# A two-layer vision tower: late rankings, layer 1's attention with its second pair beside the first, and another order of the feed-forward's pieces and end

## The chip, the cores and the metric

The kernel runs on one core of one Trainium2 chip. A core has a matrix engine (TensorE, PE in the profile, its weight loads are PEld), a vector engine (VectorE, DVE), a scalar engine (ScalarE, ACT), GpSimd (POOL) and SyncE (SP), which here only starts transfers. Each takes its instructions from a queue of its own and waits on semaphores for what others make. The metric is the device time of one execution in microseconds (us), as a median over runs.

## What is computed

A batch of 32 images of 3 x 256 x 256 goes through a tokenizer and two layers. All is float32; every image has N = 256 tokens of D = 256 features.

```python
h = L0_tok(x)                                  # 16 x 16 patches @ W.T + b
h = h + L0_attn(layernorm(h))                  # gated attention, relu(q k)^2
h = h + L0_ffn(layernorm(h))                   # the 127 best-ranked tokens of an image get a gelu MLP
h = h + L1_attn(layernorm(h))                  # phase memory
h = h + L1_ffn(layernorm(h))                   # experts' attention by head, two norms, two gates
```

Layer 0's feed-forward ranks each image's tokens by one weight, takes the best 127, and adds back `y * weight` at their places. Layer 1's attention makes phases for key and query, `tanh(gelu(x W1) W2) * freq * pi`, and reads a causal memory; for a fixed position it is a masked product:

```python
key_phasor = cos(key_phase) + 1j * sin(key_phase)
query_conj = cos(query_phase) - 1j * sin(query_phase)
memory     = cumsum(key_phasor[..., None] * V[:, :, None, :], axis=1)
retrieved  = real(sum(memory * query_conj[..., None], axis=2)) / sqrt(positions * K)
out        = x + layernorm(retrieved) @ Wo + bo
```

Layer 1's feed-forward works on 4 heads of 64 features with 4 experts each: causal softmax attention by head and expert, a gate over the experts, a residual, a norm, a two-layer MLP with a residual, a second norm, and a gate over the heads.

## The kernel before

The 32 images stay on the chip in `H[b]`, 128 partitions by 2 x 256. The stages follow one another: tokenizer (a), layer 0's attention (b, by pairs of images), layer 0's feed-forward (c, by quads), layer 1's attention (d, by pairs) and layer 1's feed-forward (e, by image). All matmuls go through `mm` (line 115) into one pool of eight PSUM banks, so TensorE's rows mostly carry L115; transposes have L188, L229, L482, L750 and L1254.

The order is written out by hand: `manual_schedule` makes every engine's queue follow the order of the Python calls. A stage is a loop over steps `t`, in which each piece of work of each unit is called at its own step; so work of several units is interleaved.

**Stage b's end and stage c.** `norms_c(b0)` normalizes a pair of images and makes the ranking weights `cw` (L378, VectorE). `turn_weights` (L482) turns `cw` on TensorE, and `ranks` (L389 to L400) counts ranks on VectorE and scatters the rows by GpSimd transfers. The rankings of the last two pairs fall into stage c's first two steps. Stage c takes four steps for a quad: `hidden_c` twice (16 matmuls each), `made` twice, `turn_c`, then `fetch` (GpSimd gathers result rows into `cx`, L816, two images each time) and `update` (VectorE adds them to `H`, L827, with the statistics that follow). `ORDER_C` sets the steps; `step_c(t)` calls what is due. The last quad's `fetch` and `update` fall behind stage c's loop (`END_C` = 32) and are called within stage d.

**Stage d**, a pair u in three steps: `norm_d` at 3u (VectorE, L774 to L777, tile `dx`, or `cx` for a pair that is normalized in stage c), `turn` at 3u+1 (8 transposes) and `residual_d` (GpSimd, four adds), `hidden` at 3u+2 (16 matmuls with gelu), `phases` at 3u+3 (16 small matmuls, two tanh, three VectorE steps L899 to L903 on `dz`, one sine), `match` at 3u+4 (16 small matmuls, then the causal mask on VectorE into `dat`, L919), `memory` at 3u+5, `output` at 3u+6 (16 matmuls, statistics L943, a power on GpSimd L149), `add_output` (L952) and `stats_e` at 3u+7. There are 16 pairs.

**Stage e**, an image b: six steps per image, at even steps `scores` (TensorE) with `weights` (VectorE adds the causal mask L1100, ScalarE the exponential L1102), at odd ones `values` (three calls, at 11, 13 and 15 of an image's own steps; copied out at L1118). All else of an image is cut into pieces `prep` and `post`, and the table `PIECES` gives each its step from the image's beginning; `EARLY` puts two ahead of the weights. The pieces of `post`: 0 to 2 the experts' gate (L1163 to L1177, then two multiplications on GpSimd, L1180), 3 the mixed sum (L1185 to L1188), 15 and 4 its squares and norm (ScalarE, L1193, GpSimd L1131 and L1132), 5 the scaling (L1198), 6 transposes (`fxT`), 16 a count of zeros, 7 the first MLP matmul, its relu `hx`, and four transfers that put `fxT` and `hx` into `both` (SyncE, L1215 and L1217), 8 the second matmul (`W`, L1226), 9 and 10 the second norm, 11 the scaling `enorm` and head gate (L1234 to L1241), 12 and 13 transposes there and back, 14 the output `fout` (L1259, L1263) with its transfer (L1264). Most of these tiles have one buffer. `LAST` sets how many steps the loop runs on after the last image has begun.

The loop before, in the few lines that set the order:

```python
for t in range(3 * (B // 2 - 1) + 8):          # stage d
    ...
    do(1, turn)
    do(7, add_output)
    ...
    if 3 <= t <= 5:
        step_c(END_C + t - 3)
...
for t in range(-1, 6 * (B - 1) + LAST):        # stage e
```

Of the kernel before, what the change touches and what calls it, by code (L numbers as in the profile page):

```python
# [33 lines left out]
F32 = mybir.dt.float32  # L34
# [6 lines left out]
P = 128  # L41
B, N, D = 32, 256, 256
NC = N // P
# [36 lines left out]
def vit_tower(tc, a, out):  # L80

    nc = tc.nc
# [62 lines left out]
    def pow_rstd(o, var):  # L145

        n = o.shape[1]
        nc.gpsimd.tensor_scalar(o, var, 1.0, 1e-5, ALU.mult, ALU.add)
        nc.gpsimd.tensor_tensor(o, o, minus_half[:, 0:n], ALU.pow)  # L149
# [254 lines left out]
    with (  # L404
# [71 lines left out]
        def turn_weights(b0):  # L476
            p = bank()
            for j in range(2):
                w = normed_c[b0][j][1]
                for c in range(NC):  # L480
                    o = j * N + c * P
                    nc.tensor.transpose(p[:, o : o + P], w[:, c : c + 1].to_broadcast([P, P]), ident)  # L482
            return p

        def ranks(b0, p):
            for j in range(2):
                rank_c(b0 + j, *normed_c[b0][j], p[:, j * N : (j + 1) * N])
# [301 lines left out]
    with region_c:  # L789
        st_d = new_stats("d")  # L790

        def hidden_c(b0, s, half):
            if half == 0:
                s.hT = p2.tile([P, 8, 4 * P], F32, name="hT")
            for m in range(4 * half, 4 * half + 4):
                p = bank()
                for k in range(2):
                    mm(p, w1[:, k, m * P : (m + 1) * P], s.xsel[:, k, :], k == 0, k == 1)
                nc.scalar.activation(s.hT[:, m, :], p, AF.Gelu_apprx_tanh, bias=col("b1", m))

        def made(b0, s, half):
            for j in range(2 * half, 2 * half + 2):
                p = bank()
                for m in range(8):
                    mm(p[:, 0:D], s.hT[:, m, j * P : (j + 1) * P], w2[:, m, :], m == 0, m == 7)
                y = p2.tile([P, D], F32, name="cy", bufs=4)
                nc.vector.tensor_tensor(y, p[:, 0:D], row_c("b2"), ALU.add)
                nc.sync.dma_start(results[b0 + j][:], y)

        def fetch(b0, s, half):  # L810
            s.y = s.y if half else []
            for b in range(b0 + 2 * half, b0 + 2 * half + 2):
                y = px.tile([P, NC, D], F32, name="cx", bufs=8)
                for c in range(NC):
                    k = b * NC + c
                    nc.gpsimd.indirect_dma_start(  # L816
                        y[:, c, :], None, results[b][:], bass.IndirectOffsetOnAxis(rank_of[:, k : k + 1], 0)
                    )
                s.y.append(y)

        def update(b0, s, half):
            for j in range(2 * half, 2 * half + 2):
                b = b0 + j
                st, rs, i = at(st_d, b)
                for c in range(NC):
                    k = b * NC + c
                    nc.vector.scalar_tensor_tensor(  # L827
                        H[b][:, c, :], s.y[j][:, c, :], w_kept[:, k : k + 1], H[b][:, c, :], ALU.mult, ALU.add
                    )
                    stats(st, i, c, H[b][:, c, :])  # L830
            pow_rstd_of(st_d, b0 + 2 * half, 2)

        ORDER_C = ((0, hidden_c, 0), (1, hidden_c, 1), (2, made, 0), (-1, turn_c, 0), (-8, first_ranks, 0),
                   (3, made, 1), (4, fetch, 0), (5, fetch, 1), (5, update, 0), (6, update, 1))

        def step_c(t):
            for at_step, do, j in ORDER_C:
                u, r = divmod(t - at_step, 4)  # L840
                if r == 0 and 0 <= u < B // 4 and (u > 1 or do is not first_ranks):
                    do(4 * u, quads[u], j)

        END_C = 4 * (B // 4 - 1) + 4
        pairs = [Pair() for _ in range(B // 2)]
        preparing = prepare()
        for t in range(END_C):
            if t < 2:
                ranks(B - 4 + 2 * t, turn_weights(B - 4 + 2 * t))
            if t == 0:  # L850
                norms_c(B - 2)
                residuals_c(B - 2)
            if t == END_C - 2:
                norm_d(0, pairs[0], px, "cx", 8)
            step_c(t)
            if t >= 8:
                next(preparing, None)
        passing.close()
# [5 lines left out]
    with (  # L864
# [4 lines left out]
            s.xT = p2.tile([P, 2, 2 * N], F32, name="dxT")  # L869
            transposed(s.xT, s.xs, copy_split)  # L870

        def hidden(b0, s, i):

            g = p2.tile([P, 2, 2 * N], F32, name=f"dg{i}")
            for m in range(2):
                p = bank()
                for k in range(2):
                    mm(p, (wk1, wq1)[i][:, k, m * P : (m + 1) * P], s.xT[:, k, :], k == 0, k == 1)
                nc.scalar.activation(g[:, m, :], p, AF.Gelu, bias=bias_d[:, 2 * i + m : 2 * i + m + 1])
            s.g = (s.g if i else []) + [g]  # L880

        def phases(b0, s):

# [48 lines left out]
                nc.scalar.copy(m.rearrange("p k n -> p (k n)"), p)  # L932
                s.m.append(m)

        def output(b0, s):
            st_m = spool.tile([P, 2 * NC, 2], F32, name="d_st")
            s.po = []
            for q in range(2 * NC):
                m, c, p = s.m[q // NC], q % NC, bank()
                for k in range(2):  # L940
                    mm(p, m[:, k, c * P : (c + 1) * P], wvo[:, k, :], k == 0, k == 1)
                six = spool.tile([P, 6], F32, name="six")
                nc.vector.bn_stats(six, p[:, 0:D])  # L943
                nc.vector.bn_aggr(st_m[:, q, :], six)
                s.po.append(p)
            s.rs = spool.tile([P, 2 * NC], F32, name="d_rs")
            pow_rstd(s.rs, st_m[:, :, 1])

        def add_output(b0, s):
            for q, p in enumerate(s.po):  # L950
# [8 lines left out]

        for t in range(3 * (B // 2 - 1) + 8):
            def do(step, which, *more):
                u, r = divmod(t - step, 3)
                if r == 0 and 0 <= u < B // 2:
                    which(2 * u, pairs[u], *more)

            do(1, turn)
            do(7, add_output)
            if t != 4:  # L970
                do(4, match)
            do(7, stats_e)
            do(1, residual_d)
            do(2, hidden, 0)
            if t == 5:
                match(0, pairs[0])
            do(2, hidden, 1)
            do(5, memory)
            do(3, phases)
            if t:  # L980
                do(0, norm_d, p8, "dx", 4)
            do(6, output)
            if 3 <= t <= 5:
                step_c(END_C + t - 3)
    right_d.close()
    passing_x.close()
    by_hand.close()
# [2 lines left out]
    with (  # L990
# [166 lines left out]
        def post(b, im, i):  # L1157
# [113 lines left out]


        images = [Image() for _ in range(B)]
        SCORES, VALUES, LAST = 6, 11, 46
        EARLY = ((32, post, 9), (22, post, 15))
        PIECES = (
            (0, prep, 0), (42, post, 12), (30, post, 16), (18, post, 1),
            (25, post, 5), (7, prep, 7), (31, post, 8), (19, post, 2),
            (26, post, 6), (44, post, 13), (2, prep, 2),
            (45, post, 14), (33, post, 10), (21, post, 3),  # L1280
            (28, post, 7), (40, post, 11),
            (23, post, 4), (17, post, 0), (-1, prep, -1),
        )

        def pieces(t, table):
# [6 lines left out]
        with order:  # L1292
            for t in range(-1, 6 * (B - 1) + LAST):
                active = [(images[b], t - 6 * b) for b in range(B)]
                if t % 2 == 0:
                    step = [(im, i - SCORES) for im, i in active if SCORES <= i < SCORES + 6]
                    made = [(im, i // 2 - 2) for im, i in active if i in (4, 6)]
                    for im, k in step:
                        scores(im, k)
                        scores(im, k + 1)  # L1300
                    for im, hp in made:
                        experts(im, hp)
                    for im, i in active:
                        if i == 6:
                            head_values(im)
                    pieces(t, EARLY)
                    for im, k in step:
                        weights(im, k)
                        weights(im, k + 1)
                    for im, hp in made:  # L1310
                        experts_out(im)
                pieces(t, PIECES)
                for im, i in active:
                    if i in (VALUES, VALUES + 2, VALUES + 4):
                        values(im, (i - VALUES) // 2)


        n_bad = p1.tile([P, 2], F32, name="n_bad")
# [390 lines left out]
```

## Time and profile before

The time is 2002.92 us (median of three runs, 2000.7 to 2003.91); the profiled execution has a span of 2000.3 us at a mean TensorE clock of 0.984.

| engine | busy us | share of the span |
|---|---|---|
| PE | 1942.6 | 97% |
| DVE | 1289.7 | 64% |
| ACT | 824.6 | 41% |
| POOL | 722.7 | 36% |

The stages on the trace's clock: a to about 196, b to about 692, c to about 934, d to about 1285, e to the end. In the loop of stage e an image takes about 20.5 us.

In a list of waits, the row names who waited, for whose work, then the time in all, how often, and the longest. In an answer in order of time, the columns are start, duration, engine, line, operation, output and inputs, shapes and count; a bracket at the end holds the idle time before it and what ended it. In a table by stretches, each engine has its busy time with the number of instructions, then come the mean granted TensorE clock, the share of the transfers' engines and the GB/s. "PEclk" on the page is that clock in tenths, in 40 equal slices.

### The profile page before, as it was taken

The page shows a single profiled execution, that of the slowest core. Times are in us where ns is not written, and L with a number is a line of the kernel's source. Part 1 is how long each engine was busy: PE and PEld are TensorE (multiplying, and loading weights), DVE is VectorE, ACT ScalarE, POOL GpSimd, SP SyncE. Part 2 cuts the span into 40 slices and gives each one's busy share as a digit, 9 for nine tenths or more (in the row PEclk, how much of TensorE's full clock was granted, in tenths as well). Part 3 has the DMA queues.
Part 4 walks back from the last instruction along what each step waited for, and adds up shares of the span by engine and source line. Part 5 has one row for each costly group of instructions (what it writes and reads, how often), then busy time and mean ns, then how long its engine had stood idle before and what let it go on. Part 6 is the DMA issues. An engine that isn't in the chain of part 4 may idle for free.

```text
span 2000.3 us, 37646 instructions
## 1 busy us (share of the span) xinstructions
PE 1942.6 (97%) x15108; PEld 1373.5 (69%) x15108; DVE 1289.7 (64%) x3605; ACT 824.6 (41%) x1549; POOL 722.7 (36%) x692
## 2 busy tenths in 40 slices
PE   9999999999999999998999999999999999999984
PEld 7886676666767666765555555577777777777762
DVE  2334566656565735334655646567889998989986
ACT  0002222222121111122344444377777777777761
POOL 1223234334342334234333342214443444444353
PEclk9999999999999999999999999999999999999995
DMA  8540000000000232121000000001222121212211
GB/s 297 158 142 1 0 19 29 24 14 22 11 21 11 85 98 80 52 68 50 11 1 1 0 1 1 6 18 44 49 53 57 44 65 44 60 49 58 52 50 54
DMA packets 69812, 95.08 MB, mean 48 GB/s; under 512 B 8576, under 2 KB 51200, under 8 KB 69248
## 3 DMA queue, kind: packets, MB, share of 16 engines
q1 hardware_dynamic: 62912, 75.04, 13.2%
q0 software_dynamic: 6144, 16.79, 2.7%
q8 instruction: 121, 1.98, 0.4%
q10 hardware_dynamic: 576, 0.79, 0.1%
q14 instruction: 59, 0.48, 0.1%
HBM read 46.45 MB, written 20.97 MB: 34 GB/s over the span
## 4 chain that ended last, share of the span: by engine, by line
PE 94%; DVE 4%; DMA 1%; ACT 0%; issue 0%; SPq 0%; POOL 0%; ACTq 0%; DVEq 0%
PE bank L115 89%; PE bank L750 2%; PE bank L188 1%; PE bank L1254 1%; DMA both<-hx 0%; DMA patch<-in_patches_dram 0%; PE bank L229 0%; PE bank L482 0%; DVE fout L1263 0%; DVE ctmp L375 0%; DVE two L1185 0%; DVE fout L1259 0%; DVE ctmp L391 0%; DVE ctmp L389 0%; DVE six L123 0%
## 5 line engine op out<-in xcount | busy, mean ns | idle before, releaser
L1102 ACT ACTIVATE et<-bank 128x512 f32<-128x512 f32 x384 | 202.4, 599 | 59.0 <-DVE bank L1100 58.5
L115 PEld LDWEIGHTS bank<-ev,et 128*64 128x64 f32 x6144 | 198.2, 137 | 33.2 <-ACT et L1102 20.6
L115 PE MATMUL bank<-ev,et 128*64 128x74 f32 (+1 forms) x6144 | 211.1, 226 | 0.0
L1100 DVE TENSOR_TENSOR bank<-bank,w_tri 128x256 f32<-128x256 f32 (+1 forms) x384 | 173.3, 514 | 56.1 <-PE bank L115 54.4
L1180 POOL TENSOR_TENSOR eo<-eo,gate 128x1024 f32<-128x1024 f32 x64 | 121.9, 1926 | 215.9 <-DVE gate L1177 203.2
L115 PE MATMUL bank<-g,sx 64*128 64x512 f32 (+1 forms) x512 | 191.0, 502 | 1.4 <-ACT g L1060 1.4
L115 PE MATMUL bank<-g,sw 64*128 64x512 f32 (+1 forms) x512 | 189.9, 502 | 0.1
L115 PE MATMUL bank<-tokW,patch 128*128 128x256 f32 x768 | 166.7, 380 | 2.8 <-DMA patch<-in_patches_dram 2.8
L115 PEld LDWEIGHTS bank<-tokW,patch 128*128 128x128 f32 x768 | 146.0, 190 | 23.8 <-DMA tokW<-in_tokW_dram 3.3
L115 PE MATMUL bank<-bxT,w_wuv 128*128 128x512 f32 x300 | 131.4, 592 | 0.0
L1132 POOL TENSOR_TENSOR hv<-hv,minus_half 128x8 f32<-128x8 f32 x64 | 119.5, 1868 | 5.3
L1118 ACT COPY eo<-bank 128x286 f32<-128x286 f32 x256 | 97.4, 423 | 57.9 <-PE bank L115 51.4
L115 PE MATMUL bank<-wvo,dm 128*128 128x512 f32 x256 | 114.0, 598 | 0.0
L115 PE MATMUL bank<-w_wo,gT 128*128 128x256 f32 x512 | 113.1, 379 | 0.0
L115 PE MATMUL bank<-xsel,w_w 128*128 128x512 f32 x256 | 113.1, 600 | 0.0
L115 PE MATMUL bank<-attn,bv 128*128 128x256 f32 x512 | 113.1, 379 | 0.0
L115 PE MATMUL bank<-w_w,hT 128*128 128x256 f32 x512 | 113.1, 379 | 0.0
L115 PEld LDWEIGHTS bank<-attn,bv 128*128 128x128 f32 x512 | 97.2, 190 | 19.6 <-issue 6.9
L123 DVE BATCH_NORM_STATS2 six<-h 128x6 f32<-128x256 f32 x256 | 105.5, 412 | 4.4
L1131 POOL TENSOR_SCALAR hv<-ranges 128x8 f32<-128x8 f32 x64 | 39.1, 611 | 190.1 <-DVE ranges L1193 189.9
L115 PEld LDWEIGHTS bank<-w_w,hT 128*128 128x128 f32 x512 | 96.7, 190 | 15.8 <-issue 3.4
L115 PEld LDWEIGHTS bank<-w_wo,gT 128*128 128x128 f32 x512 | 97.2, 190 | 13.2
(265 smaller groups left out, 3739.0 us busy)
## 6 DMA issues: line engine op xcount, KB each, us to landing
patch<-in_patches_dram SPq DMA_DIRECT2D x31, 768.0 KB
sw<-sx SPq DMA_DIRECT2D x64, 128.0 KB
both<-fxT SPq DMA_DIRECT2D x64, 128.0 KB
both<-hx SPq DMA_DIRECT2D x64, 128.0 KB
out_dram<-fout SPq DMA_DIRECT2D x32, 256.0 KB
cs<-ranked SPq DMA_DIRECT2D x32, 128.0 KB
results<-cy SPq DMA_DIRECT2D x32, 128.0 KB
w_w<-in_w_dram SPq DMA_DIRECT2D x2, 1024.0 KB
```

Source lines behind the costliest of these rows:

```text
L115: nc.tensor.matmul(o, lhsT, rhs, start=first, stop=last)
L123: nc.vector.bn_stats(six, x)
L188: nc.tensor.transpose(p[:, o : o + P], x[:, c, k * P : (k + 1) * P], ident)
L750: nc.tensor.transpose(p[:, o : o + P], x[:, c, k * P : (k + 1) * P], ident)
L1100: nc.vector.tensor_tensor(own, own, over(tri, [P, n_e, P], 1), ALU.add)
L1102: nc.scalar.activation(t, p, AF.Exp)
L1118: nc.scalar.copy(im.o[:, c * NH + n, 0:OC], p[:, 0:OC])
L1131: nc.gpsimd.tensor_scalar(v, x, 1.0 / HD, 1e-8, ALU.mult, ALU.add)
L1132: nc.gpsimd.tensor_tensor(v, v, minus_half, ALU.pow)
L1180: nc.gpsimd.tensor_tensor(im.mix[k], im.mix[k], over(im.gate[:, :, 2 * k : 2 * k + 2], [P, NC * NH, 2, HD], 3), ALU.mult)
L1254: nc.tensor.transpose(im.po[:, o : o + P], im.fT[:, k, c * P : (c + 1) * P], ident)
```

## The change

It has four parts. In stage c, the rankings of the last two pairs come after the step's other work, not ahead of it. In stage d, the second pair is normalized with the first in stage c, and turned right behind the first pair's hidden matmuls; the first `match` lies within the second pair's hidden matmuls; the last quad's fetches and updates move from steps 3 to 5 to steps 6 to 8. At stage d's end, the last pair's `match` comes between the third and fourth output matmuls of the pair ahead, whose sum comes after the match. In stage e, pieces 5, 6 and 7 come one, one and two steps sooner, pieces 11 to 14 six steps sooner (another image's turn of the same place); the loop stops when the last image's first values are made, and what is left follows in an order of its own, `END`, whose entries are (images back from the last, piece). It is meant to fill places where TensorE waits, and to shorten the end, where it has little to do.

```diff
         for t in range(END_C):
-            if t < 2:
-                ranks(B - 4 + 2 * t, turn_weights(B - 4 + 2 * t))
             if t == 0:
                 norms_c(B - 2)
                 residuals_c(B - 2)
             if t == END_C - 2:
-                norm_d(0, pairs[0], px, "cx", 8)
+                for u in range(2):
+                    norm_d(2 * u, pairs[u], px, "cx", 8)
             step_c(t)
+            if t < 2:
+                ranks(B - 4 + 2 * t, turn_weights(B - 4 + 2 * t))
...
-        for t in range(3 * (B // 2 - 1) + 8):
+        NP = B // 2
+        for t in range(3 * (NP - 1) + 8):
...
-            do(1, turn)
-            do(7, add_output)
+            last = t == 3 * NP + 1
+            if t != 4:
+                do(1, turn)
+            if not last:
+                do(7, add_output)
             if t != 4:
                 do(4, match)
+            if last:
+                output(B - 4, pairs[NP - 2], (3,))
+                add_output(B - 4, pairs[NP - 2])
             do(7, stats_e)
-            do(1, residual_d)
+            if t != 4:
+                do(1, residual_d)
             do(2, hidden, 0)
-            if t == 5:
+            if t == 2:
+                do(2, hidden, 1)
+                turn(2, pairs[1])
+            elif t == 5:
+                do(2, hidden, 1, (0,))
                 match(0, pairs[0])
-            do(2, hidden, 1)
+                do(2, hidden, 1, (1,))
+            else:
+                do(2, hidden, 1)
             do(5, memory)
             do(3, phases)
-            if t:
+            if t == 5:
+                residual_d(2, pairs[1])
+            if t > 3:
                 do(0, norm_d, p8, "dx", 4)
-            do(6, output)
-            if 3 <= t <= 5:
-                step_c(END_C + t - 3)
+            if t == 3 * NP:
+                output(B - 4, pairs[NP - 2], (0, 1, 2))
+            else:
+                do(6, output)
+            if 6 <= t <= 8:
+                step_c(END_C + t - 6)
...
-        SCORES, VALUES, LAST = 6, 11, 46
+        SCORES, VALUES, LAST = 6, 11, 12
         EARLY = ((32, post, 9), (22, post, 15))
         PIECES = (
-            (0, prep, 0), (42, post, 12), (30, post, 16), (18, post, 1),
-            (25, post, 5), (7, prep, 7), (31, post, 8), (19, post, 2),
-            (26, post, 6), (44, post, 13), (2, prep, 2),
-            (45, post, 14), (33, post, 10), (21, post, 3),
-            (28, post, 7), (40, post, 11),
+            (24, post, 5), (0, prep, 0), (36, post, 12), (30, post, 16), (18, post, 1),
+            (25, post, 6), (7, prep, 7), (31, post, 8), (19, post, 2),
+            (38, post, 13), (2, prep, 2), (26, post, 7),
+            (39, post, 14), (33, post, 10), (21, post, 3),
+            (34, post, 11),
             (23, post, 4), (17, post, 0), (-1, prep, -1),
+        )
+        END = (
+            (1, 1), (1, 2), (4, 12), (2, 5), (3, 16), (0, 0), (2, 6), (1, 3), (1, 15),
+            (1, 4), (0, 1), (3, 8), (3, 9), (0, 2), (1, 5), (4, 13), (4, 14), (3, 10),
+            (2, 7), (2, 16), (1, 6), (0, 3), (0, 15), (2, 8), (1, 7), (0, 4), (2, 9),
+            (3, 11), (0, 5), (2, 10), (1, 16), (0, 6), (1, 8), (1, 9), (0, 7), (1, 10),
+            (3, 12), (2, 11), (3, 13), (3, 14), (0, 16), (0, 8), (0, 9), (2, 12), (1, 11),
+            (2, 13), (1, 12), (0, 10), (2, 14), (0, 11), (1, 13), (1, 14), (0, 12), (0, 13),
+            (0, 14),
         )
...
+            for j in range(1, 3):
+                values(images[-1], j)
+            for back, i in END:
+                post(B - 1 - back, images[B - 1 - back], i)
```

`hidden` takes the halves it makes (`ms`) and `output` the quarters (`qs`), so that they can be called in parts.

More of the change, by code (lines that the diff above doesn't have):

```diff
@@ L870, in turn, with hidden @@
             transposed(s.xT, s.xs, copy_split)
-        def hidden(b0, s, i):
-            g = p2.tile([P, 2, 2 * N], F32, name=f"dg{i}")
-            for m in range(2):
+        def hidden(b0, s, i, ms=(0, 1)):
+            if ms[0] == 0:
+                s.g = (s.g if i else []) + [p2.tile([P, 2, 2 * N], F32, name=f"dg{i}")]
+            g = s.g[i]
+            for m in ms:
                 p = bank()
@@ L879, in hidden @@
                 nc.scalar.activation(g[:, m, :], p, AF.Gelu, bias=bias_d[:, 2 * i + m : 2 * i + m + 1])
-            s.g = (s.g if i else []) + [g]
         def phases(b0, s):
@@ L933, in memory, with output @@
                 s.m.append(m)
[L935 to L938, printed above, removed]
+        def output(b0, s, qs=range(2 * NC)):
+            if qs[0] == 0:
+                s.st, s.po = spool.tile([P, 2 * NC, 2], F32, name="d_st"), []
+            for q in qs:
                 m, c, p = s.m[q // NC], q % NC, bank()
@@ L943, in output @@
                 nc.vector.bn_stats(six, p[:, 0:D])
-                nc.vector.bn_aggr(st_m[:, q, :], six)
+                nc.vector.bn_aggr(s.st[:, q, :], six)
                 s.po.append(p)
-            s.rs = spool.tile([P, 2 * NC], F32, name="d_rs")
-            pow_rstd(s.rs, st_m[:, :, 1])
+            if len(s.po) == 2 * NC:
+                s.rs = spool.tile([P, 2 * NC], F32, name="d_rs")
+                pow_rstd(s.rs, s.st[:, :, 1])
         def add_output(b0, s):
@@ L958, in stats_e @@
             pow_rstd_of(st_e, b0, 2)
-        for t in range(3 * (B // 2 - 1) + 8):
+        NP = B // 2
+        for t in range(3 * (NP - 1) + 8):
             def do(step, which, *more):
                 u, r = divmod(t - step, 3)
-                if r == 0 and 0 <= u < B // 2:
+                if r == 0 and 0 <= u < NP:
                     which(2 * u, pairs[u], *more)
-            do(1, turn)
-            do(7, add_output)
+            last = t == 3 * NP + 1
[3 more added lines that the diff above has]
+                do(7, add_output)
             if t != 4:
                 do(4, match)
+            if last:
+                output(B - 4, pairs[NP - 2], (3,))
+                add_output(B - 4, pairs[NP - 2])
             do(7, stats_e)
-            do(1, residual_d)
+            if t != 4:
+                do(1, residual_d)
             do(2, hidden, 0)
-            if t == 5:
+            if t == 2:
[3 more added lines that the diff above has]
+                do(2, hidden, 1, (0,))
                 match(0, pairs[0])
-            do(2, hidden, 1)
+                do(2, hidden, 1, (1,))
+            else:
+                do(2, hidden, 1)
             do(5, memory)
             do(3, phases)
-            if t:
+            if t == 5:
+                residual_d(2, pairs[1])
+            if t > 3:
                 do(0, norm_d, p8, "dx", 4)
-            do(6, output)
-            if 3 <= t <= 5:
-                step_c(END_C + t - 3)
+            if t == 3 * NP:
[4 more added lines that the diff above has]
+                step_c(END_C + t - 6)
     right_d.close()
```

## The prediction

> **What bounds the kernel now.** I read the page first, then TensorE's waits, then busy time by stretch, then the order of time around each wait. The page says that TensorE is the bound, at full clock nearly everywhere:
>
> ```profile
> PE 1942.6 (97%) x15108; PEld 1373.5 (69%) x15108; DVE 1289.7 (64%) x3605; ACT 824.6 (41%) x1549; POOL 722.7 (36%) x692
> PEclk9999999999999999999999999999999999999995
> ```
>
> No edit removes a matmul, so all there is to win is TensorE's idle time and the half-clock stretches beside it. TensorE's waits (in all, times, longest):
>
> ```profile
> PE bank L750 <- DVE lg L1236: 15.7, 5, 6.2
> PE bank L188 <- DVE dx L777: 6.9, 2, 4.6
> PE bank L115 <- DMA both<-hx: 6.6, 4, 2.4
> PE bank L482 <- DVE cw L378: 3.6, 2, 2.5
> PE bank L115 <- DVE dat L919: 2.8, 1, 2.8
> ```
>
> Rows 1 and 3 are the feed-forward's end; 2, 4 and 5 are single places, and the diff aims at each. Busy time by stretch (PE first, PEclk eighth):
>
> ```profile
> 945.00:975.00 30.00, 23.94 (x88) 13.02 (x89) 22.34 (x54) 11.35 (x15) 11.30 (x12) 0.83 0.07 18
> 975.00:1270.00 295.00, 295.00 (x1239) 165.33 (x1239) 166.38 (x488) 125.68 (x168) 103.70 (x112) 1.00 0.00 1
> 1345.00:1924.00 579.00, 579.00 (x8875) 451.01 (x8872) 517.81 (x1420) 440.65 (x959) 245.45 (x167) 1.00 0.21 52
> 1924.00:2001.00 77.00, 39.28 (x474) 29.50 (x472) 55.63 (x145) 22.84 (x47) 29.42 (x22) 0.69 0.19 53
> ```
>
> The middles of both stages have no idle TensorE at all: nothing to win there, only to lose. The waits in order of time:
>
> ```profile
> 701.60 0.40 PE L482 MATMUL bank<-ident,cw 128*128 128x128 f32 x2 [2.54 <-DVE cw L378]
> 948.70 0.80 PE L188 MATMUL bank<-ident,dx 128*128 128x128 f32 x2 [4.57 <-DVE dx L777]
> 951.86 1.65 PE L188 MATMUL bank<-ident,dx 128*128 128x128 f32 x6 [2.35 <-DVE dx L777]
> 1273.76 4.55 PE L115 MATMUL bank<-dat,dx 128*128 128x256 f32 x16 [2.77 <-DVE dat L919]
> ```
>
> **The skill beside the trace.** "TensorE: Matmul & The Clock Gate", Part 1, "What's actually happening", puts the clock at half after about one idle window of 3413 ns. The trace agrees: the 16 matmuls of 7.03 us take 8.73 after the 701.6 wait. So a wait costs more than itself. "PSUM — Partial Sum Buffer", "Engine vs sequencer instructions", calls the vector, scalar and GpSimd queues strict FIFO; here VectorE's update at 760.65 waits for its gather with other work behind it. "GPSIMD Engine Reference", "Specifications", says that GpSimd shares SBUF interfaces with VectorE; the 128x2 `d_one` of 0.17 us took 1.26 beside an L786 add.
>
> **A, rankings later.** Today turn_weights(30) needs norms_c(30), which VectorE does after ranks(28): waits 2.54 + 1.09, and hidden_c 8.73 for 7.03. After: norms_c stands first and needs 3.2 us from the power's end at 696.7, so `cw` is there near 700; the transposes come after the second half of hidden_c, near 706 (691.4 + 2 x 7.03 + 0.7). What the move costs: ranks(30) (4.6 us) begins near 707 for 703.6, and its four scatters end near 717 for 718.2, against a made() that starts near 707 for 711.9. GpSimd's first fetch so comes 10 us into made() for 6.5, and its rows land (4.3 us, see B) by 18.6 us, where update() ended at 19.4 before: hidden. Gain 3.6 + 1.7 = 5.3 us; 3.6 if the half clock came for another reason.
>
> **B, second pair with the first.** From hidden(0)'s end (942.2) to phases of pair 1 (966.4) are 24.2 us. The work between, at full clock: turn 1.0, phases 1.9, hidden 7.1, match 1.5, memory 2.7 = 14.2. So 10.0 to win: 6.9 idle and 3.1 of half clock. The new order fills it: turn(1) needs norms made in the previous stage (4.7 us on a VectorE with room), and match(0) has 5.3 us of hidden(1) ahead of it where its angles take 4.9 (944.13 to 949.02).
>
> But quad 7's fetches and updates move from t = 3..5 to 6..8, into the steady loop. Its free place on VectorE, and the gather's latency:
>
> ```profile
> 1032.35 0.88 DVE L899 TENSOR_SCALAR dz<-dturn,cols 128x512 f32<-128x512 f32 x2 [7.62 <-ACT dturn L897]
> 757.53 0.95 POOL L816 DMA_INDIRECT cx<-results,rank_of  x1 [0.30 <-issue]
> 761.80 0.48 DVE L827 SCALAR_TENSOR_TENSOR h<-cx,w_kept,h 128x256 f32<-128x256 f32 x1
> ```
>
> 7.6 us free against 8 x 1.05 = 8.4 of updates; and a gather is there 4.3 us after GpSimd takes it (757.53 to 761.80). Count from phases(1). GpSimd, in order: output's power to +11.4; four gathers of 1.26 to +16.5; stats_e's power to +17.7; residual's four adds to +22.9; four gathers, the last begun at +26.7. VectorE's update(7, second half), written at t = 8, so ends at +26.7 + 4.3 + 1.1 = +32.1. Behind it in the same queue are the angles of pair 2, due at +23.9, then norm_d(3): ready at 32.1 + 2.8 + 2.1 = +37.0. TensorE wants that in turn(3) at +29.9. A new wait of 7 us, with some 3 of half clock as for the 6.9 above: 10. Between 0 (gathers in time) and 12 (the adds hold up VectorE besides) I take 10. B nets 0: the wait moves from 949 to about 981 on the new clock (951 + 29.9).
>
> **C, last match within outputs.** memory(15) waits for `dat`, which VectorE does after add_output(14), itself behind the last output's statistics. After: match(15) comes three outputs (5.3 us) after phases(15)'s 1262.35, at 1267.66, its angles are there at 1267.36, the mask runs beside the fourth output, and memory starts without waiting. Gain 2.77 + (4.55 - 2.78) = 4.5 us. Bounds 2 to 5.
>
> **D, pieces sooner, in the full loop.** Same work, other places; cost nil if each input is there. Post 5 wants L1132's result: made at 1628.6, asked at 1629.7. Post 11: made 1643.9, asked 1644.9. Post 6's transposes: asked at 1631.65, input at 1630.3. About 1 us to spare each, and VectorE idles 1.46 us per image besides. I take 0; bound 0.3 x 31 = 9 us.
>
> **E, the end.** The loop stops with image 31's first values; the other two follow at once: ready near 1935 instead of 1944.5, so its first piece (L1163) comes at 1940.3 for 1949.8. Posts 11 to 14 come six steps earlier, so one image's worth (3.5 us of VectorE) is already done. One image's pieces cost VectorE 1.0 (post 0) + 0.6 (1) + 0.8 (2) + 2.6 (3) + 0.6 each (4, 5, 16, 10) + 0.8 (8) + 1.5 (11) + 2.1 (14) = 11.8 us, from their rows in the loop. Still to do from image 31 down: 11.8 + 10.8 + 6.2 + 5.6 + 2.1 = 36 us, plus some 3 under GpSimd's two 1.9 us multiplications, and the 1.1 of L1125. From 1936 alone that gives 1976, 18 us early. Waits stretch it: I walked the 55 pieces with this trace's durations, every queue in order. VectorE waits 12 us, mostly because image 29's four `both` transfers stand on SyncE behind image 27's `out`, whose sum comes late (as today: `out` at 1944.55, `both<-fxT` at 1945.12, though fxT was ready at 1942.9). Image 31's mixed sum (L1185) falls at 1954.6 for 1960.4, its W matmuls at 1973.8 for 1976.5, its last scaling (L1234) at 1982.4 for 1988.6, its last sum at 1988.0; the same walk of the old order gives 1994.4, where the trace has 1993.97:
>
> ```profile
> 1993.28 0.69 DVE L1263 TENSOR_TENSOR fout<-fout,h 128x512 f32<-128x512 f32 x1
> ```
>
> Gain 6.4 us. It is 5 if `fout`, of one buffer, also waits for its transfer; 12 if the SyncE waits were absent.
>
> **Sum.** 2002.9 - 5.3 - 0 - 4.5 - 0 - 6.4 = 1986.7 us.
>
> **Rivals.**
> 1. The moved fetches hide: B keeps its 10, 1976.7. For it: 7.6 us free on VectorE nearly fit the 8.4. Against: one queue, and 4.3 us per gather.
> 2. The ends give less: the new wait costs 12, the end only 2, C 2: 2002.9 - 5.3 + 2 - 2 - 2 = 1995.6. For it: 36 us of VectorE at the end don't shrink. Against: the walk fits the old end.
> 3. Slower: D's spare 1 us isn't there, and each image loses 0.8 us: 1986.7 + 25 = 2011.5. For it: VectorE is 89% busy in the loop (517.81 of 579). Against: 1.46 us idle per image would swallow it first.
>
> **Chances.** Forecast 0.6, rival 1 0.2, rival 2 0.13, rival 3 0.07. The range from 1974.5 to 1996 holds the first three with their bounds. Faster by over 0.2% (below 1998.9): 0.91; within: 0.03; slower: 0.06, all from rival 3 but a little.
>
> **What would show it.** Right: no wait at L482; none for `dx` near 940; one wait of about 7 us for `dx` near 981, and before it VectorE's L827 waiting some 6 us for `cx` (from +20.7 to +27.2); no `dat` wait; 20.5 us per image in the loop; from the loop's last scores (now 1928.8) to the last sum 59 us instead of 65. Wrong if the `dx` wait is missing (then 10 us faster), if TensorE shows waits inside the loop, or if the last image's first piece isn't sooner.

## The result, and the profile after

The changed kernel takes 1985.88 us (median of four runs, 1985.12 to 1986.59) against 2001.81 us for the kernel before beside it: a ratio of 0.992, with a 95% interval of 0.9902 to 0.9937. It was forecast at 1986.7.

The page of the changed kernel, busy time and granted clock:

```profile
PE 1929.2 (97%) x15108; PEld 1372.8 (69%) x15108; DVE 1308.7 (66%) x3605; ACT 821.1 (41%) x1549; POOL 721.3 (36%) x692
PEclk9999999999999999999999999999999999999996
```

TensorE does the same 15108 matmuls in 13.4 us less, and its mean granted clock is 0.987 for 0.984, so part of what was won was half clock, stretches in which the granted clock is about 0.5. Its waits (in all, times, longest):

```profile
PE bank L115 <- DMA both<-hx: 9.3, 4, 7.3
PE bank L750 <- DVE sm_m L1165: 7.8, 1, 7.8
PE bank L188 <- DVE dx L777: 5.4, 2, 5.2
PE bank L1276 <- ACT foT L1268: 4.8, 4, 2.0
PE bank L750 <- DVE er L1220: 4.4, 2, 2.3
PE bank L115 <- ACT g L1082: 3.5, 5, 0.7
```

No L482 row and no `dat` row is left. The waits for `dx` come to 5.4 us instead of 6.9, at another place. The other long ones belong to the end, where 15.7 us for the head gate and 6.6 for `both` gave way to 9.3 for `both` and 12.2 in front of `er`'s transposes (the rows of `sm_m` and `er`).

Busy time by stretch, with the columns as shown for before:

```profile
945.00:975.00 30.00, 30.00 (x137) 17.39 (x136) 17.92 (x49) 14.46 (x21) 13.01 (x14) 1.00 0.07 18
975.00:1000.00 25.00, 19.55 (x62) 10.66 (x61) 16.07 (x47) 5.95 (x9) 11.53 (x15) 0.86 0.08 22
1330.00:1910.00 580.00, 577.39 (x8892) 457.06 (x8892) 523.94 (x1438) 442.25 (x966) 246.74 (x169) 1.00 0.21 53
1910.00:1985.00 75.00, 33.06 (x464) 24.27 (x462) 52.36 (x135) 21.11 (x44) 27.93 (x22) 0.71 0.18 48
```

The stretch that was 6 us short of full (945 to 975) is full, and the one behind it, full before, is now short of 5.4 us at a clock of 0.86.

For a closer reading I divide each trace at the same points: the first patch matmuls that waited for their transfer (8.82 us before, 8.51 after), the first `hidden` of stage d, the `phases` of the fourth pair and of the last (252.06 us from one to the other in every kernel), stage e's first transposes, the last scores, and the end of the last sum on VectorE. Stretches in us, each from the one execution that was profiled, while the time is the median of all runs; the kernels of the experiments stand with them:

| kernel | time | patch to first hidden | to 4th phases | last phases to e | e to last scores | to last sum |
|---|---|---|---|---|---|---|
| before | 2001.81 | 926.30 | 73.29 | 24.55 | 641.92 | 67.03 |
| after | 1985.88 | 920.19 | 72.32 | 20.04 | 640.66 | 64.10 |
| fetches early | 1980.53 | 921.86 | 63.79 | 20.04 | 640.65 | 63.85 |
| `fout` twice | 1980.02 | 920.18 | 71.36 | 20.04 | 640.54 | 58.70 |
| `out` later | 1982.28 | 920.19 | 71.22 | 20.04 | 640.66 | 61.63 |
| stage e only | 1997.55 | 924.47 | 72.57 | 24.39 | 640.49 | 63.26 |
| all three | 1969.68 | 920.18 | 64.57 | 20.04 | 640.58 | 55.49 |
| fetch early, update late | 1981.79 | 920.18 | 65.84 | 20.04 | 640.77 | 65.61 |
| pairs only | 1998.60 | 924.48 | 71.25 | 24.55 | 642.59 | 66.93 |
| rankings only | 1995.44 | 920.19 | 73.59 | 24.56 | 641.69 | 66.92 |
| multiplications together | 1973.63 | 920.18 | 63.44 | 20.05 | 640.54 | 60.35 |
| pieces only | 2002.62 | 926.37 | 73.21 | 24.55 | 640.53 | 69.06 |
| match only | 1996.54 | 927.82 | 72.95 | 20.04 | 642.35 | 67.20 |

From before to after the five columns give -6.1, -1.0, -4.5, -1.3 and -2.9: 15.8 us of the 15.9 measured.

### The profile page after: what moved, and what is told of

The parts are those of the page before. It is cut to its first block, busy times and chain, and to the rows that moved or that the text cites. A ratio compares the mean times of both kernels' runs of the same rounds, so it can differ in the third digit from the quotient of the medians.

```text
span 1984.1 us, 37645 instructions
## 1 busy us (share of the span) xinstructions
PE 1929.2 (97%) x15108; PEld 1372.8 (69%) x15108; DVE 1308.7 (66%) x3605; ACT 821.1 (41%) x1549; POOL 721.3 (36%) x692
```

## Experiments on the second pair and the fetches

**Fetches back.** The changed kernel with

```diff
-            if 6 <= t <= 8:
-                step_c(END_C + t - 6)
+            if 3 <= t <= 5:
+                step_c(END_C + t - 3)
```

> The changed kernel with the last quad's fetches and updates back at steps 3 to 5 of stage d; the new order of the first two pairs stays. Theory (the moved fetches make the wait for dx in turn(3) and take back what the pair order won): the 5.2 us wait and its half clock near 985 go, no other wait of over 1 us comes, and the time falls by about 9 us, to 1977. Rival (there is no free place for the updates anywhere, they only move): VectorE then holds up the first match's mask or the second pair's phases, a new wait of 3 to 9 us stands between 940 and 975, and the time stays within 3 us of 1986.

Measured: 1980.53 us (1977.75 to 1980.8), ratio to before 0.9888 (0.9873 to 0.9903), 5.4 us below the changed kernel. The stretch in question is 8.5 us shorter, has no `dx` wait and no new wait of over 1 us: the theory's mechanism, and nothing for the rival. The time is 3.5 us above the 1977 of the theory. In the profiled run 2.7 us of that were lost at its very start: the patch came 1.05 us later, and a half-clock stretch in the first 20 us cost 1.7. The other three runs have no trace, so for the median this is not shown.

What the edit removes is this, VectorE in the changed kernel:

```profile
971.15 0.18 DVE L124 BATCH_NORM_AGGREGATE st_d<-six 128x2 f32<-128x6 f32 x1
976.57 0.48 DVE L827 SCALAR_TENSOR_TENSOR h<-cx,w_kept,h 128x256 f32<-128x256 f32 x1 [5.23 <-DMA cx<-results,rank_of]
...
981.50 0.85 DVE L901 TENSOR_SCALAR dz<-dturn,cols 128x512 f32<-128x512 f32 x2
...
985.69 0.73 DVE L777 TENSOR_SCALAR dx<-h,rs_d,d_one 128x256 f32<-128x256 f32 x2
```

and its cause on GpSimd:

```profile
971.87 1.27 POOL L787 TENSOR_TENSOR h<-h,add_row 128x512 f32<-128x512 f32 x1
973.30 1.05 POOL L816 DMA_INDIRECT cx<-results,rank_of  x1 [0.16 <-issue]
```

GpSimd is in its residual adds until 973.1 and takes the second half's first gather only then. VectorE stands for 5.23 us in front of the rows, with the angles (L901) and the next pair's norm (L777) behind it in its queue. TensorE pays:

```profile
985.12 0.80 PE L188 MATMUL bank<-ident,dx 128*128 128x128 f32 x2 [5.20 <-DVE dx L777]
```

**Gathers early, updates late.** Are the late gathers at fault or the updates' own 8.4 us on a VectorE that has 7.6 free?

```diff
-            if 6 <= t <= 8:
-                step_c(END_C + t - 6)
+            if 3 <= t <= 4:
+                fetch(B - 4, quads[B // 4 - 1], t - 3)
+            if 7 <= t <= 8:
+                update(B - 4, quads[B // 4 - 1], t - 7)
```

> The changed kernel with the last quad's gathers back at steps 3 and 4 of stage d, while the updates on VectorE stay at steps 7 and 8. Theory (the wait near 985 comes from gathers that GpSimd reaches late, behind its power and its four residual adds, not from the updates' own time): the rows lie ready, VectorE's 8.4 us of updates nearly fit the 7.6 us free in one pair, so a wait for dx of at most 1 to 2 us is left and the time is 1977 to 1979. Rival (VectorE has no room for the updates in the steady loop, whoever fetches when): a wait for dx of 4 to 5 us stays, and the time stays within 2 us of 1986.

Measured: 1981.79 us (1978.37 to 1986.08), ratio 0.9896 (0.9882 to 0.9911). The time alone, 4.1 us below the changed kernel with wide runs, would leave it open; the trace doesn't. The stretch takes 65.84 us, 6.5 less than in the changed kernel, and the place of the long wait now reads:

```profile
982.67 1.09 PE L188 MATMUL bank<-ident,dx 128*128 128x128 f32 x6 [0.39 <-DVE dx L777]
```

So it was the gathers behind GpSimd's adds; the updates' time costs these transposes about 1 us (2.0 us for 1.0 in the version with the fetches back). A new wait of 1.5 us for the first pair's sine, near 945, takes part of the gain. Most of it is one operation of the chain to the sine, which took 2.58 us where it takes 1.23 in the changed kernel and with the fetches back. GpSimd's second pair of residual adds, which now comes behind the gathers and has no updates to wait for, began beside it:

```profile
942.04 2.58 DVE L905 TENSOR_TENSOR dz<-dz,dn 128x1024 f32<-128x1024 f32 x1
942.25 1.28 POOL L786 TENSOR_TENSOR h<-h,cx 128x512 f32<-128x512 f32 x1
```

ScalarE's L899, ahead of it, began 0.5 us later after the phases than in the changed kernel; why stays open.

**Only the pairs and the fetches**, on the kernel before, the core of the edit:

```diff
-                norm_d(0, pairs[0], px, "cx", 8)
+                for u in range(2):
+                    norm_d(2 * u, pairs[u], px, "cx", 8)
...
+            if t == 2:
+                do(2, hidden, 1)
+                turn(2, pairs[1])
+            elif t == 5:
+                do(2, hidden, 1, (0,))
                 match(0, pairs[0])
+                do(2, hidden, 1, (1,))
...
-            if 3 <= t <= 5:
-                step_c(END_C + t - 3)
+            if 6 <= t <= 8:
+                step_c(END_C + t - 6)
```

> The kernel before with the order of stage d's first two pairs and the move of the last quad's fetches as in the change, and nothing else of it. Theory (the new wait near 985 eats what the pair order wins): from the first hidden matmuls of stage d to the fourth pair's phases 72.3 us as in the whole change, against 73.3 before, so 0 to 1 us faster, not to be told from no change. Rival (part of the loss near 985 comes from the other parts of the change): 5 us or more faster.

Measured: 1998.6 us (1997.41 to 2002.0), ratio 0.9985 (0.9978 to 0.9993): 3.0 us faster, between theory and rival. In the profiled run 1.8 us of the difference lie in the first stretch, where the two kernels don't differ (see the rankings below). The trace has the `cw` and `dat` waits of before and the new `dx` wait of 5.4 us. The first stretch of stage d takes 71.2 to 72.3 us in the four kernels with this order of pairs and late gathers, 72.6 to 73.6 in the five with the old order: on the mean 71.5 against 73.1, so 1.6 us won, not 0 and not 10.

## Experiments on the rankings and the last match

**Rankings only**, on the kernel before:

```diff
-            if t < 2:
-                ranks(B - 4 + 2 * t, turn_weights(B - 4 + 2 * t))
...
             step_c(t)
+            if t < 2:
+                ranks(B - 4 + 2 * t, turn_weights(B - 4 + 2 * t))
```

> The kernel before with the rankings of the last two pairs after the step's other work, and nothing else. Theory (the two waits for cw of 3.6 us go, the transposes run 0.5 us shorter, and a half-clock stretch worth 1.7 us goes in those executions that have one there; one of the runs above had the waits without it): 4 to 6 us faster, 1996 to 1998. Rival (the rankings come later and hold up the first fetches, so that made or the loop of stage c waits instead): 2 us faster or less.

Measured: 1995.44 us, ratio 0.9965 (0.9952 to 0.9979), 6.1 us faster, just above the upper end. In the trace the two waits are gone. VectorE now waits for the rows of the later fetches (L827, 4.2 us in two waits between 690 and 800, for 0.2 before), but TensorE has no new wait in stage c. How much of the gain is certain is seen in the kernels that kept the old rankings. The first stretch takes 926.3 in two of them and 924.5 in two others, with identical instructions. The difference is the granted clock behind the same 2.54 us wait. Before, and then the kernel with stage e's edits only, the clock in the eighth column:

```profile
700.00:710.00 10.00, 7.30 (x16) 3.34 (x17) 9.12 (x30) 1.38 (x2) 4.94 (x5) 0.83 0.64 200
```

```profile
700.00:710.00 10.00, 7.41 (x20) 3.51 (x21) 7.28 (x32) 2.06 (x3) 2.70 (x3) 1.00 0.58 180
```

Of the five executions with this wait, three had the half clock behind it and two did not ("match only" had it too, beside 1.5 us lost at its start). So the part is worth 4.3 us in all five (3.6 of waits, 0.5 of the eight transposes, which run in two groups of 0.60 us where they took 1.67 in pieces behind their inputs, at full clock both times, and a little), and 1.8 more in the three. The Trainium skill, "TensorE: Matmul & The Clock Gate", Part 1, "What's actually happening", says that the window of 3413 ns is free-running, which fits a cost that comes in some executions and not in others. It puts half clock after at least one idle window, though, and here the trace doesn't agree as fully as the prediction said: no wait in this place is as long as a window (2.54 us, and 1.10 after 0.4 us of transposes), and the single wait of 2.77 us for `dat` was followed by half clock in all five kernels that have it (4.39 to 4.56 us for 16 matmuls that take 2.78). How idle TensorE has to be for how long stays open.

**Match only**, on the kernel before:

```diff
+            if last:
+                output(B - 4, pairs[NP - 2], (3,))
+                add_output(B - 4, pairs[NP - 2])
...
-            do(6, output)
+            if t == 3 * NP:
+                output(B - 4, pairs[NP - 2], (0, 1, 2))
+            else:
+                do(6, output)
```

> The kernel before with the last pair's match between the third and fourth output matmuls of the pair ahead, and nothing else. Theory: from the last phases to the first transpose of stage e 21.35 us instead of 25.87, the wait for dat gone, 4.5 us faster, 1997.0. Rival (2.8 us of waiting go, but the half clock stays): 2.8 us, 1998.8.

Measured: 1996.54 us (1994.87 to 2000.48), ratio 0.9976 (0.9968 to 0.9984), 5.2 us faster; the stretch is 20.04 us instead of 24.55 in every kernel with this part, 4.5 us. Theory, not rival: the wait goes and the half clock with it.

## Experiments on stage e

**Stage e only**, on the kernel before, with the changed `PIECES` and `END`:

```diff
-        SCORES, VALUES, LAST = 6, 11, 46
+        SCORES, VALUES, LAST = 6, 11, 12
...
+            for j in range(1, 3):
+                values(images[-1], j)
+            for back, i in END:
+                post(B - 1 - back, images[B - 1 - back], i)
```

> The kernel before with the changed stage e alone (PIECES, LAST, END). Theory (the parts do not touch each other: the end 2.9 us, the loop and its filling 1.2 us): 4.1 us below the kernel before, near 1997.7. Rival (part of the end's gain is owed to the earlier stages, or the differences in the loop are noise): 2.5 us or less.

Measured: 1997.55 us, ratio 0.9977 (0.9969 to 0.9985), 4.2 us faster, as the theory had it. Each of the four parts alone brings its stretch within 1.1 us of what the whole change has there, so they hardly touch each other. Their times alone add up to 18.5 us for 15.9 together, which the intervals (3.5 us to either side for the whole change) don't tell apart.

**Pieces only**, on the kernel before, the entries that move:

```diff
-            (25, post, 5), (26, post, 6), (28, post, 7),
-            (40, post, 11), (42, post, 12), (44, post, 13), (45, post, 14),
+            (24, post, 5), (25, post, 6), (26, post, 7),
+            (34, post, 11), (36, post, 12), (38, post, 13), (39, post, 14),
```

> The kernel before with the new table PIECES alone, the loop running on to its old end and no order of its own there. Theory (the filling and the loop give 1.2 us through the pieces; of the end's gain of 2.9 to 3.8 us less than half comes from pieces 11 to 14 having been done six steps sooner, the rest from END and the earlier stop): 1.5 to 3 us faster than before, 1998.8 to 2000.3. Rival (the loop's end order does nothing, the pieces' places do all): 4 us or more faster, as stage e's whole edit.

Measured: 2002.62 us, ratio 1.0004 (0.9996 to 1.0012): nothing. Theory and rival were both wrong. The filling and the loop get their 1.4 us, but the end gets 2.0 longer (69.06 for 67.03): the sooner pieces alone make the old end's order worse. So `END` and the earlier stop are worth 5 to 6 us (69.1 to 63.3 or 64.1), and what the pieces cost at the end hides part of it.

**`fout` twice.** The changed kernel with

```diff
-                y = p1.tile([P, NC, D], F32, name="fout")
+                y = p2.tile([P, NC, D], F32, name="fout")
```

> The changed kernel with two buffers for fout. Theory (the last sum waits 4 us for the transfer of the sum ahead of it, which reads the only fout): the DMA wait at the last L1281 goes and the last sum comes 3 to 4 us sooner, 1982 to 1983. Rival (the wait only takes the place of another, for TensorE's transposes or the last head gate, so the last sum is bound by the chain through W): within 1 us of 1986.

Measured: 1980.02 us (1978.56 to 1980.93), ratio 0.9891 (0.9876 to 0.9906), 5.9 us below the changed kernel; the end alone is 5.4 shorter, more than the 3 to 4 expected. The chain that ended last of the changed kernel ends so (start, duration, what):

```profile
1971.43 0.60 DVE fout L1285
1972.06 4.33 DMA out_dram<-fout
1976.48 0.70 DVE fout L1281
1977.20 0.69 DVE fout L1285
```

The last product stands for 4 us until the sum ahead of it has been carried out. This transfer took 4.33 us from issue to landing; the median for `fout` on the page is 2.5. Two smaller things go with it. The product before it waited 0.28 us in the same way, and between that product and its sum VectorE has the cast of the flag at the kernel's end, which is written behind the order made by hand and waited for TensorE:

```profile
1971.29 0.15 DVE L1367 CAST flag<-bank 1x1 int32<-1x1 f32 x1 [0.99 <-PE bank L115]
```

With two buffers the flag comes behind that sum in the trace. From the last scaling to the last sum it is then 5.9 us instead of 10.7. In the kernel before, the last sums came 5.3 us apart, and the last product, 3.9 us behind the sum ahead, waited for TensorE and not for a transfer; moved together they do.

**`out` later.** The changed kernel with `(4, 14)`, image 27's `out`, after `(2, 7)`:

```diff
-            (1, 4), (0, 1), (3, 8), (3, 9), (0, 2), (1, 5), (4, 13), (4, 14), (3, 10),
-            (2, 7), (2, 16), ...
+            (1, 4), (0, 1), (3, 8), (3, 9), (0, 2), (1, 5), (4, 13), (3, 10),
+            (2, 7), (4, 14), (2, 16), ...
```

> The changed kernel with one entry of END moved: image 27's out (piece 14) comes after image 29's piece 7, so that its transfer no longer stands ahead of the four transfers into both on SyncE. Theory (SyncE's order costs at the end): image 29's transfers are issued about 10 us sooner, TensorE's 7.3 us wait for both falls to under 2 us, and the last sum comes 2 to 3 us sooner, 1983 to 1984. Rival (VectorE's own work and GpSimd's multiplications set the last images' pace; the W wait is filled by another): within 1 us of 1986, with the idle time of TensorE showing under another name.

Measured: 1982.28 us (1980.87 to 1983.82), ratio 0.9899 (0.9884 to 0.9914), 3.6 us below; the end is 2.5 shorter, as expected, and the time somewhat below the 1983 to 1984. SyncE in the changed kernel:

```profile
1914.12 25.92 SPq L1286 DMA_DIRECT2D out_dram<-fout  x2
1940.27 1.11 SPq L1237 DMA_DIRECT2D both<-fxT  x2
```

The second of the two `out` entries waits for its sum until 1939.6, and image 29's `both` is issued behind it although `fxT` was there at 1926.0. In the version with `out` later:

```profile
1925.91 1.10 SPq L1237 DMA_DIRECT2D both<-fxT  x2
```

The W wait falls from 7.3 us to under 1. TensorE's waiting in front of `er`'s transposes becomes 14.3 us for 12.2, though, and of the 14 us by which this transfer starts sooner the end keeps 2.5.

**All three edits together**, the three diffs above in one kernel:

> The changed kernel with the last quad's fetches and updates at steps 3 to 5, two buffers for fout, and image 27's out after image 29's piece 7, all three. Theory: stage d gives its 8.5 us in full; at the end the two edits (5.4 and 2.5 us alone) do not add up, since both shorten the same last chain, and give 6 to 7 together: 1970.5 to 1971.5, no wait for fout's transfer, no W wait of over 2 us. Rival (the end is bound by VectorE's own work once one of them is gone): the end gives no more than the 5.4 of the two buffers, 1972 or above.

Measured: 1969.68 us (1969.5 to 1970.45), ratio 0.984 (0.9826 to 0.9853): 16.2 us below the changed kernel, of which stage d 7.75 and the end 8.6. It beats both kernels. The theory missed on both sides: stage d keeps a wait of 0.9 us for the first pair's sine and doesn't give its 8.5, and the two edits at the end give more than the 5.4 and 2.5 that they give alone, not 6 to 7. Why more isn't shown. The rival's time was wrong too, but its chain shows why the end gives no more by such means, a part of the last 20 us:

```profile
1948.33 0.62 DVE junk L1066 x2
1948.97 0.22 DVE n_bad L1357
1949.19 0.19 DVE ey L1248
1949.45 0.43 DVE ey L1248
1949.88 0.60 DVE enorm L1256
1950.48 0.11 DVE lg L1258
```

From 1944.7 to 1956.2 every step is VectorE's own work but for short ones marked "issue", of which the longest takes 0.57 us: there the end is now bound by VectorE.

**Multiplications together.** On that kernel, image 31's pieces 0, 1, 2 ahead of image 30's piece 3:

```diff
-            (1, 1), (1, 2), (4, 12), (2, 5), (3, 16), (0, 0), (2, 6), (1, 3), (1, 15),
-            (1, 4), (0, 1), (3, 8), (3, 9), (0, 2), (1, 5), ...
+            (1, 1), (0, 0), (1, 2), (4, 12), (2, 5), (3, 16), (0, 1), (0, 2), (2, 6), (1, 3), (1, 15),
+            (1, 4), (3, 8), (3, 9), (1, 5), ...
```

> The kernel with all three edits, and the last image's pieces 0, 1 and 2 ahead of the image before's piece 3, so that GpSimd's two multiplications for image 31 follow those for image 30 at once, ahead of that image's power. Theory (the last image's mixed sum waits for GpSimd, which ends its multiplications at 1931 with a break of 6.7 us ahead of them): they end near 1926, image 30's power comes about 1 us later, the small operations on VectorE no longer stand beside a multiplication, and the last sum comes 2 to 4 us sooner: 1966 to 1968. Rival (image 30's chain, now 1 us later, or VectorE's own work sets the end): within 1 us of 1969.7.

Measured: 1973.63 us (1970.82 to 1975.1), ratio 0.9858 (0.9843 to 0.9873): 4 us slower than without, and the end 4.9 longer, where the theory had it 2 to 4 faster and the rival within 1 us. The multiplications do end at 1926.6, but image 30's mixed sum now lies beside them. VectorE in this kernel:

```profile
1922.62 2.23 DVE L1209 TENSOR_TENSOR er<-two 128x512 f32<-128x512 f32 x1
1924.88 2.28 DVE L1210 TENSOR_TENSOR er<-er,res 128x512 f32<-128x512 f32 x1
```

Elsewhere each takes 0.69. The Trainium skill, "GPSIMD Engine Reference", "Specifications", names VectorE instructions with two SBUF inputs among those that contend with GpSimd; these two have them, and GpSimd multiplies from 1921.5 to 1926.6. Image 30's `er` is scaled 4.7 us later after the last scores (1930.65 - 1905.00 for 1926.92 - 1905.93), where I had taken 1; 3.1 of it are these two operations. Of the rival's two reasons the first fits, image 30's chain, with a size that it had not foreseen; no run takes the overlap alone away.

## Why the prediction was right

**A, rankings later: 5.3 forecast, 6.1 between the two profiles.** Both waits went, and none came for them on TensorE. VectorE does stand 3.7 us in front of the later rows, which the prediction had as hidden; it had the time. The surplus is mostly 0.5 us of transposes, forgotten in the sum. Of what was forecast, 1.7 of half clock (1.8 measured) is a matter of the execution: without it the part is worth 4.3.

**B, the second pair: 0 forecast, 1.0 between the profiles, 1.6 on the mean.** This was the step with the most at stake, and its mechanism held: phases of pair 1 came 10.1 us sooner (21.20 us from the first hidden for 31.28), the wait began at 979.9 (forecast about 981), before it L827 waited 5.2 us for `cx` (forecast some 6), and the angles and the norm stood behind. TensorE's wait was 5.45 us instead of 7, with about 3.5 of half clock (a granted clock of 0.50 from 986 to 989): 9 for 10. The mis-sized term is the end of the walk. Counted from the phases of pair 1 (949.90), the norm of pair 3 ended at +36.5 for +37.0, but the first transposes began at +35.2, as soon as the first of the pair's two images was normed, where I had let them wait for both. The gather's latency mattered less: I took 4.3 us from stage c, here the rows were usable 3.3 us after GpSimd began (973.30 to 976.57), but GpSimd began the last gather 0.6 us later than in the walk, and the last update ended at +31.7 for +32.1. Rival 1, the hidden fetches, is what the kernel could have had: 8.5 us.

**C: 4.5 forecast, 4.5 measured**, in every kernel that has it.

**D: 0 forecast, 1.3 won** in the filling and the loop, in spite of three new waits of 0.72 us in it, a small case of what the prediction had named as a sign of being wrong. They fall on every eighth image. VectorE's range check (L1147, L1148, 1.1 us) stands some 7 us ahead of each; that it causes them was not tried. An image takes 20.46 us for 20.54 (eight images from one range check to the next: 163.7 for 164.3), so "nothing to win there", read from a TensorE without idle time, was not quite true.

**E, the end: 6.4 forecast, 2.9 won.** This is the term that was wrong. It is 3.5 us short, and A, B and D together are 3.1 us over: that the total came within 1 us is luck. The walk of the end was good almost to its last step. Counted from the start of the last scores, the last image's mixed sum came at 27.0 us (forecast 27.7), its W matmuls at 45.1 (46.9), its last scaling at 53.4 (55.5), the last sum at 64.1 (61.1). The walk was 2.1 us too slow up to the last scaling, and then 5.1 us too fast: from there to the last sum it has 5.6 us, the trace 10.7. What failed is the case that I named and priced at 1.4 us, `fout` waiting for its transfer: it costs 4.0 us as a wait, and the end is 5.4 shorter when it is taken away. The waits on SyncE stood where the walk had them; without them 2.5 us are won.

## What to carry to other kernels

When a change moves work of one engine into a place beside other work, walk every queue that it passes through: here a gather put behind four additions on GpSimd stopped VectorE, and through it TensorE, and took back most of what the change had won at the same place. When an order brings the ends of several units closer together, look at every tile with one buffer whose reader is a transfer: the distance between units was what had hidden it. Judge such a change by stretches between fixed points of the trace rather than by the total alone, since gains and losses of 5 us stood side by side here in a total that looked like the sum of small ones.

## What the runs showed of the hardware

The same wait of 2.54 us cost a half-clock stretch in three executions of five, a wait of 2.77 us at another place in five of five. A stretch of the same kind came in the first 20 us of 2 of the 13 profiled executions and cost 1.5 and 1.7 us. The half clock behind the 2.54 us and that of the first 20 us differ between executions of the same instructions, so neither says anything about a kernel, and each is as large as many a change. An operation of 0.69 us with two inputs in SBUF took 2.2 us beside a GpSimd multiplication, and the small L1188 (0.36 for two) took 2.95 in the changed kernel, where GpSimd multiplied from 1923.95 to 1928.1: on a chain that sets the end, a place without GpSimd's work beside it can be worth more than an earlier one.
